# Buffers of a four-layer graph network rearranged: a third residual tile, sums and 32x32 transposes in place, PSUM banks moved to the products

## The chip, the core and the metric

The kernel runs on one core of a Trainium2 chip. TensorE (PE) multiplies matrices into PSUM. VectorE (DVE), ScalarE (ACT) and GpSimd (POOL) do elementwise work; SyncE (SP) issues most transfers. The metric is device time in microseconds, the median of several executions. A profiled execution has its own time span, and is a little shorter than that median.

## The reference

128 samples of 64 tokens with 512 features go through four residual layers, in fp32. Each begins with a layer norm and a relu. Layers 0 and 2 have four heads of width 64, layer 1 has eight and a second layer norm, and layer 3 is a graph step with eight heads.

```python
# layers 0, 2 (and 1 with its own norm, 8 heads)
h = jnp.maximum(_layernorm(x, axis=-1), 0.0)
sim = jnp.einsum('bhid,bhjd->bhij', q, k) * scale       # q, k, v = h @ W
sim = jnp.where(adjacency_mask[:, None, :, :], sim, neg)
attn = jax.nn.softmax(sim, axis=-1)
x = x + (attn @ v) @ Wo + bo
# layer 3
m = embs @ map_w.T + map_b
cos_adj = (cos > THRESHOLD)                              # cosine of the heads of m
p_attn = jax.nn.softmax(where(pad, NEG, q k / sqrt(dk))) # q, k from m
sem_h = embs @ gcn_map_w.T + gcn_map_b
out = relu(((cos_adj * p_attn) @ sem_h) @ gcn_W.T / (sum + 1)); x = x + out
```

## The kernel before, in words

The tokens are cut into 16 groups of 512 (8 samples), and each layer goes over all groups. Between the layers the residual stream lies in device memory. A group's steps are: load, layer norm (`loads`, `layernorms`), turn the tokens so that features lie on partitions (`transposes`, L591), projections, scores and softmax (`front`, `scores` L957), the attention product with v (`attention` L1122, `last` L1270), the output projection, the residual sum and the store.

**Projections** are done with seven half-size products for eight (`winograd`, L700), which takes sums of the quarters of both operands. The sums of the weights are made once. The sums of the tokens are four 128x512 tiles per operand: `sums_of_b` (L356) makes B01−B00, B11 minus that, B11−B01, and B10 minus the second, on GpSimd for h and m, and on VectorE for the attention's output. In the profile they are `t<-hT`, `t<-m` (L366, L363). In the product's code they are T[0] to T[3]. The order of the products is A0·B00, A1·B10, A5·T1, A4·T0, A2·T2, A6·B11, A3·T3. Results land in PSUM tiles called `mA` (ring `ma`) and `mB`, `mC` (ring `mm`), and copies (ACT, L669) and sums (DVE, L682) bring them into SBUF.

**Turning the tokens** goes three ways. Eight groups go through TensorE (`ptr`, L609). 28 groups of layers 0 and 2 have their 32x32 blocks moved by 16 transfers each on SP (`moves`, L556, `F<-xin`), followed by VectorE's 32x32 transposes (`by_vector`, L586). 28 groups of layers 1 and 3 have the blocks copied by ScalarE and GpSimd (`turned_tokens`, L512), with a `t` tile as the staging place, then VectorE's transposes (L546).

**Softmax weights** are turned per unit of a group (`transposed`, L1014): eight 32-partition copies on ScalarE from E to F (L1021), and one VectorE transpose from F to pt (L1026). Then the attention product `po` (64x64 quarters of the array) can run.

**Residuals** (`residuals`, L1056): two halves of a group are loaded to `xres` tiles; GpSimd adds the bias (L1071) and the first product terms `u` (L1087, L1092), VectorE the others (L682), and SP stores them (L1112).

**The order.** Each engine executes one fixed list of instructions, in order; an instruction waits for semaphores of what it reads and of what it overwrites. The list is written when the program is built: each part of the work is a generator that yields an engine and an assumed duration (`pe`, `dve`, `act`, `pool`, `quads`), and `Order.run` (L138) takes next the one that could start first. DRAIN is the assumed time of a change between 64x64 quarters and the full array. A `Ring` or `Bank` with n buffers lets a new tile begin when an older one is released, in the plan as on the chip. So durations and numbers of buffers decide the order on every engine, SP's queue too.

**PSUM** has eight banks: `sc` (scores, one tile of two banks), `ma` 2, `mm` 2, and `tr` 2 for the transposes `ptr`.

Of the kernel before, what the change touches and what calls it, by code (L numbers as in the profile page):

```python
# [24 lines left out]
NEG_L3 = -1e10 * 8  # L25

DRAIN = 0.085


class Event:
# [24 lines left out]
class Stream:  # L74
# [14 lines left out]
    def quads(self):  # L89
        return self.op[3:] == ("quads",)  # L90
# [138 lines left out]
def gnn_stack(ctx: ExitStack, tc: tile.TileContext, a: dict, out: bass.AP):  # L229
# [10 lines left out]
    def bank(tag, n, shape, dtype=F32):  # L240
        return Bank(od, ctx.enter_context(tc.tile_pool(name=tag, bufs=1)), n, shape, dtype, tag)
# [4 lines left out]
    dram = ctx.enter_context(tc.tile_pool(name="dram", bufs=1, space=bass.MemoryType.DRAM))  # L246
    r_w = ring("w", 4, [P, 7, 2, H])
    r_xin = ring("xin", 2, [P, TB, D])
    r_xres = ring("xres", 2, [P, 2, D])
    r_u = bank("u", 4, [P, D])  # L250
    r_h = ring("h", 2, [P, NC, TB * P])
    r_t = bank("t", 3, [P, NC, 2, H])
    r_qk = ring("qk", 3, [P, NC, TB * P])
    r_m = bank("m", 2, [P, NC, TB * P])
    r_v = bank("v", 2, [P, TB, D])
    r_e = ring("e", 2, [P, 16, N])
    r_f = ring("f", 1, [P, 16, N])
    r_c = ring("c", 1, [P, 2, 512], U8)
    r_pt = ring("pt", 1, [P, 16, N])
    r_adj = ring("adj", 2, [P, TB, N], U8)  # L260
    r_n0 = ring("n0", 2, [P, TB, N], U8)
    ps = bass.MemoryType.PSUM
    r_sc = ring("sc", 1, [P, 2, 512], space=ps)
    r_ma = ring("ma", 2, [P, 512], space=ps)
    r_mm = ring("mm", 2, [P, 512], space=ps)
    r_tr = ring("tr", 2, [P, NC, P], space=ps)

    xs = [[dram.tile([TB * P, D], F32, name=f"x{l}_{s}") for s in range(NG)] for l in range(3)]
    x_done = {}
# [85 lines left out]

    def sums_of_b(B, T, vector=False):  # L356

        n = T.shape[2]
        for o, i0, i1 in ((T[:, 0], B(0, 1), B(0, 0)), (T[:, 1], B(1, 1), T[:, 0]),
                          (T[:, 2], B(1, 1), B(0, 1)), (T[:, 3], B(1, 0), T[:, 1])):  # L360
            if vector:
                yield dve(0.9)
                nc.vector.tensor_tensor(o, i0, i1, ALU.subtract)  # L363
            else:
                yield pool(1.42)
                nc.gpsimd.tensor_tensor(o, i0, i1, ALU.subtract)  # L366
# [94 lines left out]

    hT, hB, h_ready, h_done, t_done = {}, {}, {}, {}, {}

    def quarters(v):

        return lambda j, k: v[:, 2 * j:2 * j + 2, k * H:(k + 1) * H]
# [45 lines left out]
    def turned_tokens(l, s):  # L512


        for half in range(2):
            yield n_ready[l, s, half]
        if (l, s) == (3, 1):
            yield o_taken
        h, h_done[l, s] = yield from r_h.new("hT")
        hT[l, s] = h  # L520
        x, xe = normed.pop((l, s))
        T, t_done[l, s] = yield from r_t.new("T")
        F = T.rearrange("p c a n -> p c (a n)")
        xv = x.rearrange("p b (c k f) -> p k c b f", c=NC, k=4)
        Fv = F.rearrange("p c (b i f) -> p i c b f", b=TB, i=4)
        blocks = [(i, k) for k in range(4) for i in range(4)]

        def part(pairs, done):
            for i, k in pairs:
                o, v = Fv[32 * k:32 * (k + 1), i], xv[32 * i:32 * (i + 1), k]  # L530
                if done:
                    yield pool(0.9)
                    nc.gpsimd.tensor_copy(o, v)
                else:
                    yield act(0.615)
                    nc.scalar.copy(o, v)  # L536
            if done:
                done.set()
        moved = od.event()
        od.spawn(part(blocks[:3], moved), 3)  # L540
        yield from part(blocks[3:], None)
        yield moved
        xe.set()
        for c in range(0, NC, 2):
            yield dve(1.25)
            nc.vector.transpose(h[:, c:c + 2, :], F[:, c:c + 2, :])  # L546
        if l == 1:
            for c in range(NC):
                yield act(0.787)
                nc.scalar.activation(h[:, c, :], h[:, c, :], AF.Identity,  # L550
                                     bias=beta[:, c:c + 1], scale=gamma[:, c:c + 1])
        hB[l, s] = (quarters(h), T, od.event())
        h_ready[l, s].set()
        return h

# [35 lines left out]
    def transposes(steps):  # L591

        for l, s in steps:
            if (l, s) in by_dma:
                h = yield from by_vector(l, s)
            elif (l, s) in turned:
                h = yield from turned_tokens(l, s)
            else:
                h, h_done[l, s] = yield from r_h.new("hT")
                hT[l, s] = h  # L600
            for half in range(0 if (l, s) in turned + by_dma else 2):
                yield n_ready[l, s, half]
                x, xe = normed[l, s]
                for t in range(2):
                    b = 2 * half + t
                    pt, pe_ = yield from r_tr.new("ptr")
                    for c in range(NC):
                        yield pe(0.115)
                        nc.tensor.transpose(pt[:, c, :], x[:, b, c * P:(c + 1) * P], ident)  # L609
                    if b == TB - 1:  # L610
                        xe.set()
                    yield act(0.6)
                    nc.scalar.copy(h[:, :, b * P:(b + 1) * P], pt)
                    pe_.set()
                if (l, s, half) == (0, 0, 0):
                    yield from has_h(l, s, h)
            if (l, s) != (0, 0) and (l, s) not in turned:
                yield from has_h(l, s, h)
            yield from sums_of_b(quarters(h), hB[l, s][1], (l, s) == (0, 0))
            hB[l, s][2].set()  # L620
            if (l, s) == (0, 0):
                first_t.set()

    def has_h(l, s, h):
        T, t_done[l, s] = yield from r_t.new("T")
        hB[l, s] = (quarters(h), T, od.event())
        h_ready[l, s].set()


# [70 lines left out]
    def winograd(A, BT, tokens_out, out_, used, begun):  # L700
# [36 lines left out]
        yield read  # L737
        for e in sums:
            yield e
        yield from product(p_, A[:, 5], T[:, 1], tokens_out, False)  # L740
        read, u2 = first(0, 1, p_)
        r_, re_ = yield from r_mm.new("mC")
        r_ = r_[:, 0:width]
        yield from product(r_, A[:, 4], T[:, 0], tokens_out, True)
        read5, c22 = first(1, 1, r_)
        yield read
        yield from product(p_, A[:, 2], T[:, 2], tokens_out, False)
        read, c22 = add(1, 1, p_, c22)
        begun.set()
        yield read5  # L750
# [1 line left out]
        c12 = second(0, 1, r_, u2)  # L752
        od.spawn(when([c12], re_), 0)
        yield read
        yield from product(p_, A[:, 3], T[:, 3], tokens_out, False)
        od.spawn(out_.alone(1, 0, p_, c22, pe_), 0)
        od.spawn(when([*every, pe_], used), 0)

# [94 lines left out]

    def k_part(s, z):
        yield from of_map("k", s, z, k_b)
        od.spawn(when([z["q_ready"], z["k_ready"]], s_ready[3, s], z["m_used"], z["T_done"]), 0)

    def sem_part(s, z):

# [12 lines left out]
    def sums_after(e, B, z, done, last):  # L872
        yield e

        T, z["T_done"] = yield from (r_w if last else r_t).new("mT_T")
        z["T"] = T = T[:, 0:NC]
        yield from sums_of_b(B, T)
        done.set()

# [77 lines left out]
    def scores(lT, rT, npair, blocks):  # L957
        S, e = yield from r_sc.new("sc")
        nb = len(blocks)
        for b, t in enumerate(blocks):  # L960
            for c in range(npair):
                if c % 2 == 0:
                    yield quads(0.235)
                col = slice((c * nb + b) * N, (c * nb + b + 1) * N)
                for g in range(2):
                    k = slice(t * P + g * N, t * P + (g + 1) * N)
                    for par in range(2):
                        r = slice(par * N, (par + 1) * N)
                        nc.tensor.matmul(S[g * N:(g + 1) * N, par, col],  # L969
                                         lT[r, c, k], rT[r, c, k], start=True, stop=True)  # L970
        return S, e
# [41 lines left out]

    def transposed(E, e):  # L1014

        F, fe = yield from r_f.new("F")
        for g in range(2):
            for i in range(2):
                for k in range(2):
                    yield act(0.587)  # L1020
                    nc.scalar.copy(F[g * N + 32 * k:g * N + 32 * (k + 1), :, 32 * i:32 * (i + 1)],  # L1021
                                   E[g * N + 32 * i:g * N + 32 * (i + 1), :, 32 * k:32 * (k + 1)])
        e.set()
        o, oe = yield from r_pt.new("pt")
        yield ("dve", 1.2, 1.0)
        nc.vector.transpose(o, F)  # L1026
        fe.set()
        return o, oe

    def masks(l, s):  # L1030

# [90 lines left out]
    def attention(l, s):  # L1122
# [8 lines left out]
        for u, blocks in enumerate(units):  # L1131
# [3 lines left out]
            for b, t in enumerate(blocks):  # L1135
                for c in range(npair):
                    if c % 2 == 0:
                        yield quads(0.235)
                    for par in range(2):
                        h = 2 * c + par  # L1140
                        for g in range(2):
# [18 lines left out]
        T, te = yield from r_t.new("oT_T")  # L1160
        if (l, s) == (2, NG - 1):
            o_taken.set()
        T = T[:, :, 0:nch, :]
        yield from sums_of_b(ov, T, True)
        yield w_ready[wkey]
        wo = W["o1"] if l == 1 else o_part(W[wkey])
# [103 lines left out]
    def last(s):  # L1270
# [3 lines left out]
        for u in range(2):  # L1274
# [5 lines left out]
            for b in range(2):  # L1280
                t = 2 * u + b
                for i in range(4):
                    yield quads(0.118)
                    for ch in range(2):
                        h = 4 * ch + i
                        c, par = h // 2, h % 2
# [96 lines left out]
```

## Time and profile before

| | |
|---|---|
| time, median of 3 | 2754.21 us (2753.09 to 2754.67) |
| span of the profiled execution | 2750.0 us |
| PE, DVE, ACT, POOL busy | 97%, 71%, 69%, 59% |
| layers, roughly | L0 to 550, L1 to 1400, L2 to 1880, L3 to 2750 us |
| one product of 128x128 weights with 256 columns (two records) | 0.43 us on PE |
| one po or score group (64 quarter records) | 1.09 us between starts |
| one GpSimd token sum, 128x512 | 1.27 us |
| one VectorE transpose, 128x1024 | 1.23 us |
| one ScalarE copy, 32x512 | 0.615 us |

A row of the page or of a timeline reads: start, duration, engine, line, operation, what it writes and reads, and in brackets the idle time before it and the event that ended it. A row of waits has the waiting engine and line, the releaser, total us, times, and the longest. The chain is followed back from the last instruction to what released it.

### The profile page before, as it was taken

The page shows a single profiled execution, that of the slowest core. Times are in us where ns is not written, and L with a number is a line of the kernel's source. Part 1 is how long each engine was busy: PE and PEld are TensorE (multiplying, and loading weights), DVE is VectorE, ACT ScalarE, POOL GpSimd, SP SyncE. Part 2 cuts the span into 40 slices and gives each one's busy share as a digit, 9 for nine tenths or more (in the row PEclk, how much of TensorE's full clock was granted, in tenths as well). Part 3 has the DMA queues.
Part 4 walks back from the last instruction along what each step waited for, and adds up shares of the span by engine and source line. Part 5 has one row for each costly group of instructions (what it writes and reads, how often), then busy time and mean ns, then how long its engine had stood idle before and what let it go on. Part 6 is the DMA issues. An engine that isn't in the chain of part 4 may idle for free.

```text
span 2750.0 us, 63860 instructions
## 1 busy us (share of the span) xinstructions
PE 2678.9 (97%) x26280; PEld 2320.6 (84%) x26280; DVE 1956.6 (71%) x2836; ACT 1889.6 (69%) x3517; POOL 1615.5 (59%) x1242
## 2 busy tenths in 40 slices
PE   7989999999999999999999999999999999999997
PEld 6878888788888888888888888888888888888876
DVE  6777987767666766776668888747776677766656
ACT  5666767677877777777566667666667766677644
POOL 4666777645444544544657677686656565565643
PEclk9999999999999999999999999999999999999998
DMA  5565654212111211112455556423222342223221
GB/s 166 134 150 138 174 140 144 97 48 79 63 47 64 78 48 60 63 66 78 114 145 143 162 148 163 140 93 96 78 65 72 81 101 64 64 71 84 68 64 48
DMA packets 396980, 267.92 MB, mean 97 GB/s; under 512 B 260496, under 2 KB 305552, under 8 KB 396688
## 3 DMA queue, kind: packets, MB, share of 16 engines
q1 hardware_dynamic: 382176, 249.37, 32.8%
q10 hardware_dynamic: 14512, 14.47, 1.6%
q8 instruction: 207, 3.39, 0.5%
q14 instruction: 85, 0.70, 0.1%
HBM read 166.77 MB, written 67.63 MB: 85 GB/s over the span
## 4 chain that ended last, share of the span: by engine, by line
PE 91%; DVE 4%; ACT 2%; DMA 1%; SPq 1%; POOL 1%; issue 1%; POOLq 0%; ACTq 0%; DVEq 0%
PE mA L652 46%; PE mC L652 23%; PE mB L652 12%; PE sc L969 5%; PE po L1144 2%; PE po L1289 1%; ACT F L1021 1%; SPq L571 1%; PE mmn L911 1%; DVE mx L986 0%; PE ptr L609 0%; DMA F<-xin 0%; ACT E L992 0%; DVE st L443 0%; DVE sc L980 0%
## 5 line engine op out<-in xcount | busy, mean ns | idle before, releaser
L1021 ACT COPY F<-E 32x512 f32<-32x512 f32 x768 | 472.6, 615 | 46.1 <-POOL E L1012 28.7
L1092 POOL TENSOR_TENSOR xres<-xres,u 128x512 f32<-128x512 f32 x192 | 255.8, 1341 | 234.1 <-ACT u L1087 203.7
L1071 POOL TENSOR_TENSOR xres<-xres,u 128x512 f32<-128x512 f32 x192 | 266.2, 1407 | 55.5 <-DMA xres<-x 33.9
L366 POOL TENSOR_TENSOR t<-hT 128x512 f32<-128x512 f32 x126 | 178.5, 1416 | 167.7 <-DVE hT L546 89.6
L459 ACT ACTIVATE xin<-xin,rs 128x512 f32<-128x512 f32 x320 | 248.5, 812 | 12.1 <-DVE rs L452 9.2
L536 ACT COPY t<-xin 32x512 f32<-32x512 f32 x364 | 224.1, 616 | 6.4
L443 DVE BATCH_NORM_STATS2 st<-xin 128x6 f32<-128x512 f32 x320 | 214.4, 670 | 8.3 <-DMA xin<-in_x 4.0
L652 PE MATMUL mA<-w_vo,t 128*128 128x128 f32 (+1 forms) x1152 | 206.0, 315 | 7.3 <-ACT u L1087 4.5
L669 ACT COPY v<-mA 128x256 f32<-128x256 f32 (+1 forms) x192 | 93.6, 488 | 168.2 <-PE mA L652 163.3
L450 POOL TENSOR_TENSOR rs<-rs,mhalf 128x2 f32<-128x2 f32 x160 | 115.6, 726 | 147.8 <-DVE rs L448 118.2
L1012 POOL TENSOR_TENSOR E<-E,sm 128x1024 f32<-128x1024 f32 x64 | 129.3, 2020 | 117.2 <-DVE sm L1010 84.1
L652 PE MATMUL mA<-t,w_qk 128*128 128x256 f32 x768 | 183.1, 380 | 2.5 <-DVE t L363 1.4
L652 PEld LDWEIGHTS mA<-w_vo,t 128*128 128x128 f32 x1152 | 164.8, 193 | 20.5 <-ACT u L1087 6.3
L366 POOL TENSOR_TENSOR t<-hT,t 128x512 f32<-128x512 f32 x126 | 175.5, 1393 | 8.0 <-DVE hT L546 4.2
L652 PE MATMUL mA<-t,w_q 128*128 128x256 f32 x744 | 179.6, 384 | 0.0
L652 PE MATMUL mA<-t,w_k 128*128 128x256 f32 x744 | 177.5, 381 | 0.0
L652 PEld LDWEIGHTS mA<-t,w_qk 128*128 128x128 f32 x768 | 144.6, 190 | 22.7 <-DVE t L363 1.6
L1006 DVE TENSOR_REDUCE sm<-E 128x16 f32<-128x1024 f32 x128 | 154.8, 1209 | 8.8 <-ACT E L999 6.7
L652 PEld LDWEIGHTS mA<-t,w_q 128*128 128x128 f32 x744 | 140.7, 191 | 20.7 <-issue 0.8
L1087 ACT COPY u<-mA 128x512 f32<-128x512 f32 x144 | 84.4, 586 | 106.9 <-PE mA L652 105.4
L652 PEld LDWEIGHTS mA<-t,w_k 128*128 128x128 f32 x744 | 140.2, 190 | 19.4
L1026 DVE STREAM_TRANSPOSE pt<-F 128x1024 f32<-128x1024 f32 x96 | 118.6, 1235 | 41.2 <-ACT F L1021 40.9
(220 smaller groups left out, 6883.5 us busy)
## 6 DMA issues: line engine op xcount, KB each, us to landing
x<-xres SPq DMA_DIRECT2D x96, 512.0 KB
xin<-x SPq DMA_DIRECT2D x96, 512.0 KB
xres<-x SPq DMA_DIRECT2D x64, 512.0 KB
F<-xin SPq DMA_DIRECT2D x448, 64.0 KB
xres<-in_x SPq DMA_DIRECT2D x32, 512.0 KB
u<-rs SPq DMA_DIRECT2D x128, 128.0 KB
xres<-x SPq DMA_DIRECT2D x64, 256.0 KB
out<-xres SPq DMA_DIRECT2D x64, 256.0 KB
```

What stands on the lines that cost most here:

```text
L366: nc.gpsimd.tensor_tensor(o, i0, i1, ALU.subtract)
L443: nc.vector.bn_stats(st, v[:, t, :])
L459: nc.scalar.activation(v[:, t, :], v[:, t, :], func, bias=rs[:, 2, t:t + 1], scale=rs[:, 0, t:t + 1])
L536: nc.scalar.copy(o, v)
L652: nc.tensor.matmul(o, l, r, start=(first and m == 0 and k == 0), stop=(k == KC - 1), skip_group_check=True)
L969: nc.tensor.matmul(S[g * N:(g + 1) * N, par, col], lT[r, c, k], rT[r, c, k], start=True, stop=True)
L1006: nc.vector.tensor_reduce(o, E, AX.X, ALU.add)
L1012: nc.gpsimd.tensor_mul(E, E, sm[:, :, None].to_broadcast([P, 16, N]))
L1021: nc.scalar.copy(F[g * N + 32 * k:g * N + 32 * (k + 1), :, 32 * i:32 * (i + 1)], E[g * N + 32 * i:g * N + 32 * (i + 1), :, 32 * k:32 * (k ...
L1026: nc.vector.transpose(o, F)
L1071: nc.gpsimd.tensor_add(xr[:, t, :], xr[:, t, :], bo[l])
L1092: nc.gpsimd.tensor_add(v, v, both(u))
```

## The change

All arithmetic stays. The tiles are placed differently.

- `xres` has three buffers instead of two.
- `sums_of_b` makes B11−B01 last, and for h and the attention's output puts it into the place of the quarter B01, which no product reads (`with_room`). `t` tiles hold three sums instead of four. For m of layer 3, whose quarters are still read, the sum goes to a tile of its own, `t2`, with one buffer, released after the k product (`k_part`).
- `turned_tokens` copies the blocks straight into h, and the 32x32 transposes run in place.
- The softmax's F and pt are one tile: the transpose runs in place, and there are two of them.
- In PSUM `tr` goes; `ma` and `mm` have three banks each, and `ptr` takes its banks from `mm`.
- The planner's assumed durations change: DRAIN .085 to .1, the quarter groups .235 to .242 and .118 to .121.

```diff
-DRAIN = 0.085
+DRAIN = 0.1
...
-    r_xres = ring("xres", 2, [P, 2, D])
+    r_xres = ring("xres", 3, [P, 2, D])
-    r_t = bank("t", 3, [P, NC, 2, H])
+    r_t = bank("t", 3, [P, 3, 2, H])
+    r_t2 = ring("t2", 1, [P, 2, H])
-    r_f = ring("f", 1, [P, 16, N])
-    r_pt = ring("pt", 1, [P, 16, N])
+    r_pt = ring("pt", 2, [P, 16, N])
-    r_ma = ring("ma", 2, [P, 512], space=ps)
-    r_mm = ring("mm", 2, [P, 512], space=ps)
-    r_tr = ring("tr", 2, [P, NC, P], space=ps)
+    r_ma = ring("ma", 3, [P, 512], space=ps)
+    r_mm = ring("mm", 3, [P, 512], space=ps)
...
-        for o, i0, i1 in ((T[:, 0], B(0, 1), B(0, 0)), (T[:, 1], B(1, 1), T[:, 0]),
-                          (T[:, 2], B(1, 1), B(0, 1)), (T[:, 3], B(1, 0), T[:, 1])):
+        for o, i0, i1 in ((T[0], B(0, 1), B(0, 0)), (T[1], B(1, 1), T[0]),
+                          (T[3], B(1, 0), T[1]), (T[2], B(1, 1), B(0, 1))):
...
+    def with_room(T, B):
+        return [T[:, 0], T[:, 1], B(0, 1), T[:, 2]]
...
-        Fv = F.rearrange("p c (b i f) -> p i c b f", b=TB, i=4)
+        Fv = h.rearrange("p c (b i f) -> p i c b f", b=TB, i=4)
...
-            nc.vector.transpose(h[:, c:c + 2, :], F[:, c:c + 2, :])
+            nc.vector.transpose(h[:, c:c + 2, :], h[:, c:c + 2, :])
...
-        hB[l, s] = (quarters(h), T, od.event())
+        hB[l, s] = (quarters(h), with_room(T, quarters(h)), od.event())
...
-                    pt, pe_ = yield from r_tr.new("ptr")
+                    pt, pe_ = yield from r_mm.new("ptr")
+                    pt = pt.rearrange("p (c n) -> p c n", c=NC)
...
-        od.spawn(when([z["q_ready"], z["k_ready"]], s_ready[3, s], z["m_used"], z["T_done"]), 0)
+        od.spawn(when([z["q_ready"], z["k_ready"]], s_ready[3, s], z["m_used"], z["T_done"], z["t2_done"]), 0)
...
-        z["T"] = T = T[:, 0:NC]
+        t2, z["t2_done"] = yield from r_t2.new("mT_T2")
+        z["T"] = T = [T[:, 0], T[:, 1], t2, T[:, 2]]
...
-                    yield quads(0.235)
+                    yield quads(0.242)
...
-        F, fe = yield from r_f.new("F")
+        F, fe = yield from r_pt.new("F")
...
-        o, oe = yield from r_pt.new("pt")
         yield ("dve", 1.2, 1.0)
-        nc.vector.transpose(o, F)
-        fe.set()
-        return o, oe
+        nc.vector.transpose(F, F)
+        return F, fe
...
-        T = T[:, :, 0:nch, :]
+        T = with_room(T[:, :, 0:nch, :], ov)
...
-                    yield quads(0.118)
+                    yield quads(0.121)
```

More of the change, by code (lines that the diff above doesn't have):

```diff
@@ L356, in sums_of_b @@
     def sums_of_b(B, T, vector=False):
-        n = T.shape[2]
-        for o, i0, i1 in ((T[:, 0], B(0, 1), B(0, 0)), (T[:, 1], B(1, 1), T[:, 0]),
-                          (T[:, 2], B(1, 1), B(0, 1)), (T[:, 3], B(1, 0), T[:, 1])):
+        for o, i0, i1 in ((T[0], B(0, 1), B(0, 0)), (T[1], B(1, 1), T[0]),
+                          (T[3], B(1, 0), T[1]), (T[2], B(1, 1), B(0, 1))):
             if vector:
@@ L522, in turned_tokens @@
         T, t_done[l, s] = yield from r_t.new("T")
-        F = T.rearrange("p c a n -> p c (a n)")
         xv = x.rearrange("p b (c k f) -> p k c b f", c=NC, k=4)
-        Fv = F.rearrange("p c (b i f) -> p i c b f", b=TB, i=4)
+        Fv = h.rearrange("p c (b i f) -> p i c b f", b=TB, i=4)
         blocks = [(i, k) for k in range(4) for i in range(4)]
@@ L625, in has_h @@
         T, t_done[l, s] = yield from r_t.new("T")
-        hB[l, s] = (quarters(h), T, od.event())
+        hB[l, s] = (quarters(h), with_room(T, quarters(h)), od.event())
         h_ready[l, s].set()
@@ L739, in winograd @@
             yield e
-        yield from product(p_, A[:, 5], T[:, 1], tokens_out, False)
+        yield from product(p_, A[:, 5], T[1], tokens_out, False)
         read, u2 = first(0, 1, p_)
@@ L743, in winograd @@
         r_ = r_[:, 0:width]
-        yield from product(r_, A[:, 4], T[:, 0], tokens_out, True)
+        yield from product(r_, A[:, 4], T[0], tokens_out, True)
         read5, c22 = first(1, 1, r_)
         yield read
-        yield from product(p_, A[:, 2], T[:, 2], tokens_out, False)
+        yield from product(p_, A[:, 2], T[2], tokens_out, False)
         read, c22 = add(1, 1, p_, c22)
@@ L754, in winograd @@
         yield read
-        yield from product(p_, A[:, 3], T[:, 3], tokens_out, False)
+        yield from product(p_, A[:, 3], T[3], tokens_out, False)
         od.spawn(out_.alone(1, 0, p_, c22, pe_), 0)
@@ L1137, in attention @@
                     if c % 2 == 0:
-                        yield quads(0.235)
+                        yield quads(0.242)
                     for par in range(2):
```

## The prediction

> **What bounds the kernel.** I read the page's busy shares, the slices and the chain that ended last, then the windows by stage, and then TensorE's waits.
>
> ```profile
> span 2750.0 us, 63860 instructions
> PE 2678.9 (97%) x26280; PEld 2320.6 (84%) x26280; DVE 1956.6 (71%) x2836; ACT 1889.6 (69%) x3517; POOL 1615.5 (59%) x1242
> ...
> PEclk9999999999999999999999999999999999999998
> ...
> PE 91%; DVE 4%; ACT 2%; DMA 1%; SPq 1%; POOL 1%; issue 1%; POOLq 0%; ACTq 0%; DVEq 0%
> ```
>
> TensorE is busy for 97% at nearly full clock, and 91% of the last chain is its own work. So only what changes TensorE's idle time, or the ends of the span, can move the time. The windows (core's share, PE busy first) say where it idles:
>
> ```profile
> 50.00:690.00 640.00, 613.04 (x5822) 539.60 (x5821) 492.69 (x734) 443.44 (x887) 414.59 (x324) 0.98 0.45 124
> 700.00:1390.00 690.00, 689.80 (x6226) 599.20 (x6225) 466.13 (x695) 517.58 (x828) 334.10 (x280) 1.00 0.21 67
> 1390.00:2080.00 690.00, 681.58 (x6634) 593.91 (x6634) 506.59 (x735) 466.11 (x965) 479.25 (x357) 1.00 0.45 124
> 2080.00:2700.00 620.00, 617.12 (x6652) 521.45 (x6650) 420.10 (x550) 407.25 (x741) 343.14 (x242) 0.99 0.28 72
> 2700.00:2750.00 50.00, 31.16 (x603) 26.52 (x602) 32.54 (x35) 22.16 (x35) 20.11 (x13) 0.79 0.26 65
> ```
>
> Layer 1 has 0.2 us idle in 690: nothing to win there. Layer 0 and its passage to layer 1 have 27 us, the passage to layer 3 8.4, the tail 19. The waits of TensorE:
>
> ```profile
> PE po L1289 <- DVE pt L1026: 10.7, 2, 5.8
> PE mC L652 <- ACT v L669: 5.8, 2, 5.1
> PE po L1144 <- DVE mv L445: 5.4, 1, 5.4
> PE mA L652 <- DVE hT L586: 5.2, 1, 5.2
> PE mA L652 <- ACT u L1087: 4.5, 1, 4.5
> ```
>
> The timeline places them. The 5.2 is at 67 us, where the instruction orders of the two kernels are still equal. At 160.37 a product waits for the copy `u`, behind softmax copies on ScalarE; at 199.95 another waits for copy `v`, behind seven such copies. At 536.74 the second attention product waits for its transposed weights (its named releaser had long ended; the transpose at 535.35 is the last):
>
> ```profile
> 526.52 1.19 DVE L1026 STREAM_TRANSPOSE pt<-F 128x1024 f32<-128x1024 f32 x1
> 529.82 1.88 ACT L1021 COPY F<-E 32x512 f32<-32x512 f32 x3 [2.69 <-DVE rs L448]
> 532.20 3.12 ACT L1021 COPY F<-E 32x512 f32<-32x512 f32 x5
> 535.35 1.25 DVE L1026 STREAM_TRANSPOSE pt<-F 128x1024 f32<-128x1024 f32 x1 [1.06 <-ACT F L1021]
> 536.74 1.98 PE L1144 MATMUL po<-pt,v 64*64 64x64 f32 x64 [5.38 <-DVE mv L445]
> ```
>
> With a single F, the eight copies of the second unit cannot begin before the first transpose has read it.
>
> **What the Trainium skill says.** "TensorE: Matmul & The Clock Gate", The mechanism: matrix multiplies keep program order, at start and end. The trace agrees: behind the po at 536.74 the next `mA` starts only at 538.66. So a late operand delays everything, and the written order is what counts. "PSUM — Partial Sum Buffer", The four PSUM rules: one matmul's output lies in one bank, 512 fp32 columns. Both kernels hold all eight; the trace cannot show the limit, but shows waits for a free product bank: `mB` 1.66 us at 189.93, `mmf` 2.25 at 1412.22. "SBUF — State Buffer", Who interferes with whom: a VectorE instruction with two SBUF inputs contends with a GpSimd one that reads SBUF. The trace agrees: the L363 sum at 155.44, beside GpSimd's E at 155.27, took 2.01 us, where its like takes 0.41. New orders may make or break such meetings; I price them in the slips below.
>
> **The change, part by part.** Instruction counts per engine and kind are equal in both programs (13206 on TensorE, 2838 VectorE, 3554 ScalarE, 1247 GpSimd, 1184 SyncE), and so are the 442 switches between 64x64 groups and full products. TensorE's own work is unchanged: 0.
>
> *In-place transposes and sums.* The same 96 + 56 VectorE transposes (1.23 us each), and the same GpSimd sums (1.27 us) to another address. No row shows the in-place form. Bounds: 0, or if it drained for 0.3 us more, 152 x 0.3 = 46 us on VectorE, which is 29% idle; on the path only where a wait already ends at such a transpose (few, under 2 us). I take 0. The sums' third and fourth change places (T3 before T2): the product with T2 comes before that with T3, so T2 comes one sum, 1.3 us, later against its product. GpSimd idles 41%, and no wait above ends at a sum: 0, or 1.3 us at a layer's start.
>
> *Third product banks, transposes moved into `mm`.* Takes away the bank waits 1.66 (189.93), 0.69 (227.78), 0.90 and 2.25 (1405, 1412) as far as order allows. In exchange the `ptr` transposes (128 records, so 8 token groups of 16; four banks in each group) share `mm` with `mB`/`mC`: each holds a bank for 0.6 us of TensorE and 0.6 of ScalarE, a third bank covers that; if not, some 0.6 us a bank, 32 x 0.6 = 19 us at the very worst. I take 0.
>
> *F and pt as two in-place buffers.* The second unit's copies can begin 5 us earlier; the two po are now 16 matmuls apart (16 x 0.43 = 6.9 us) where they were 4.
>
> *The order.* The planner's constants and buffers change what is written where. TensorE's orders agree to about 154 us; from there layer 0 is rearranged (next group's q·k product ahead of the output projection; po about 4.75 us earlier), to the passage at ~550. Layer 1 differs little, layer 2 takes on the same pattern, layer 3 is nearly equal up to its last two groups.
>
> Walk through 150–230. Removed: 4.66+1.66+5.24+0.69 = 12.25. In the new order the hT transposes come earlier on VectorE, but the fetched F lands at 153.6, leaving about 2.1 for hT and 3.0 for the same `u`: 5.1. Net −7.2.
> Passage 430–550. Removed: 1.56 (441) + 0.56 + 5.45 = 7.57; left 0.5. Net −7.1.
> Passage to layer 2, 1400–1415: 3.15 removed, I leave 1.0. Net −2.1.
> New slips in the rearranged 150–570: from 1390 to 2620 this kernel's stalls over 0.6 us sum to 11.6 us in 1230, 0.0094 per us; x 420 = +4.0.
>
> *The tail.* `t2` has one buffer, so the fourth sum of the last group waits for the product of group 14's k that reads it, and the planner now puts the score products of both units of group 14 back to back after k, before the last q. Before, they were spread through q:
>
> ```profile
> 2665.91 1.46 PE L652 MATMUL mA<-m,w_q 128*128 128x256 f32 x6
> 2667.30 1.16 PE L969 MATMUL sc<-kT,qT 64*64 64x64 f32 x64
> ...
> 2668.53 1.34 DVE L980 COPY_PREDICATED sc<-adj,negs 128x1024 f32<-128x1024 uint8 x1 [3.45 <-PE sc L969]
> ...
> 2669.91 1.22 DVE L986 TENSOR_REDUCE mx<-sc 128x16 f32<-128x1024 f32 x1
> ...
> 2671.89 1.21 DVE L996 TENSOR_TENSOR E<-sc,mx 128x1024 f32<-128x1024 f32 x1
> ```
>
> The `sc` ring stays at one buffer. The first unit waits for kT's last evacuation (about 1.05 us after 2665.9), the second for mask, maximum and subtraction (1.34+1.22+1.21 = 3.8 and hops of 0.35): about 5.2 us with nothing else allowed to pass. Also one po (1.28 us with its switches) now stands ahead of the last semantic products instead of in the idle tail. What follows them keeps its length: GpSimd's E and four adds of v (1.9 + 5.2 us), eight copies, transpose, po. So the end moves by 5.2 to 5.2 + 1.28 = 6.5, as far as the po was hidden; I take +5.7.
>
> Stores on SyncE: the residual store moves from after twelve of a group's sixteen F moves to after three, costed at 0 because F moves take 16 x 0.63 = 10 us of a 27 us group; see the second rival.
>
> Sum: −7.2−7.1−2.1+4.0+5.7 = −6.7. Span 2750.0 − 6.7 = 2743.3. The profiled run's span lies 4.2 us under the median 2754.2, so 2747.5.
>
> **Rivals.** *One for one: within 0.2%* (5.5 us, about what can be told from no change here). The new layer 0 slips as the old did: 19.8 us of stalls in its 150–550. With slips of 10 instead of 4 us, the time is 2753.5. For it: `u` still stands behind softmax copies near 160, and F still arrives at 153.6. Against it: layer 2 already runs this pattern of po and projection, with almost no stall.
>
> *Slower, by SyncE's head of line.* A store issues only when the residual is finished, and everything behind it in the queue stands; at 103.9–121.4 SyncE stood 17 us at one. Now thirteen F moves (8.2 us) and the next load of xin come behind it. Per group of layer 0 and 2 after its start (some 26) any overshoot over the slack of 27 − 10 − about 5 for other transfers = 12 us comes as TensorE waiting for hT. It cancels the gain at 6.7/26 = 0.26 us of overshoot per group, and shows as slower from (6.7 + 5.5)/26 = 0.47; at 0.65 it costs 26 x 0.65 = 16.9, which gives 2747.5 + 16.9 = 2764. For it: the third residual buffer lets the store fall later in the order. Against: only one hT wait (5.2) in all of before, at the start.
>
> *The claimed gain is larger.* The walks' 5.1 left-over and slips stay out: −6.7−9 gives 2738.
>
> *Nothing of it reaches the bound:* TensorE idles too little; then the stalls stay as they are, and the tail alone gives 2754.2 + 5.7 = 2760, the edge of slower.
>
> **Numbers.** Forecast and the larger gain: 0.45 (faster). One for one: 0.33, from 2749 to 2759. SyncE's case, or the tail with no gain before it: 0.22. Likeliest 2747.5; 8 in 10 within 2738 to 2762, from the larger gain to just inside the SyncE case. The likeliest case's own range is 2740 to 2751.
>
> **What would show it.** Right: no stall over 1 us at 530–545 and at 185–205; mm-bank waits gone; PE busy within 2 us of 2679; a gap of about 4 us between two `sc` groups near 2660 with both score groups adjacent. Wrong: waits of `mA` for hT L586 in several groups with a store ahead on SyncE (second rival); in-place transposes clearly over 1.23 us; new waits for `t`, `mm` or `v` in layer 0 worth more than 5 us.

## The result, and the profile after

The changed kernel takes 2750.03 us (median of 20 runs, 2744.29 to 2756.89) beside 2754.26 us for the kernel before (20 runs, 2749.51 to 2761.38). The ratio is 0.9987, with a 95% interval of 0.9980 to 0.9994. It is faster, by 4.2 us between the medians: less than the 0.2% at which the prediction called a difference clear, and 2.5 us over its likeliest value of 2747.5.

The page of the changed kernel: span, busy shares, granted clock and the chain.

```profile
span 2750.6 us, 63739 instructions
...
PE 2682.1 (98%) x26280; PEld 2323.4 (84%) x26280; DVE 1950.9 (71%) x2836; ACT 1885.3 (69%) x3517; POOL 1608.4 (58%) x1242
...
PEclk9999999999999999999999999999999999999998
...
PE 84%; DVE 7%; ACT 3%; POOL 3%; DMA 2%; issue 1%; SPq 0%; ACTq 0%; DVEq 0%; POOLq 0%
```

The profiled execution took 2752.83 us, 2.8 us over this kernel's median, and its span of 2750.6 us is no shorter than the 2750.0 of before. The execution profiled before was on the quick side: its span is 4.2 us under the median, where spans in the other runs are about 2 us under the time of the same execution, so it was some 2 us faster than usual (an estimate). So the two traces don't show the 4 us as a sum; they show where time was won and given back. The windows of the changed kernel, cut as those of before:

```profile
50.00:690.00 640.00, 623.87 (x5946) 549.27 (x5945) 501.90 (x746) 453.27 (x907) 419.54 (x330) 0.99 0.47 125
700.00:1390.00 690.00, 685.66 (x6187) 593.87 (x6186) 438.61 (x683) 507.13 (x803) 339.28 (x281) 1.00 0.23 74
1390.00:2080.00 690.00, 683.16 (x6641) 596.87 (x6641) 524.08 (x738) 469.84 (x981) 465.21 (x349) 1.00 0.44 118
2080.00:2700.00 620.00, 611.80 (x6613) 516.89 (x6613) 419.27 (x547) 402.23 (x733) 347.35 (x243) 0.99 0.28 71
2700.00:2750.00 50.00, 31.48 (x549) 26.38 (x547) 29.23 (x34) 20.07 (x32) 13.65 (x10) 0.82 0.25 64
```

TensorE's busy time rose from 613.0 to 623.9 of the 640 us between 50 and 690, and fell from 617.1 to 611.8 in the stretch to 2700. (Busy counts half-clock time too.) TensorE's waits now:

```profile
PE po L1272 <- DVE F L1010: 10.0, 1, 10.0
PE mA L636 <- ACT v L653: 7.0, 14, 1.6
PE sc L954 <- DVE E L981: 6.9, 4, 4.9
PE mA L636 <- DVE hT L569: 6.0, 1, 6.0
PE mA L636 <- ACT u L1070: 3.6, 3, 1.7
```

The 5.2 us for `v`, 5.4 for po and 4.5 for `u` are gone. In their place are many short waits for `v` (14 with 7.0 us) and one of 4.9 us between two score groups. The 10.0 us at the end stands where two waits made 10.7.

Two notes on counting. Single waits of TensorE are given below from start to start, less the usual spacing, except where a view beside them shows the number; the views count from the modelled end of the last record and show up to 0.2 us less. And the x of a row counts matmul records, of which a product on the full array has two: x8 is four products, and the "8 products" of an expectation below are eight records.

For an account in places, I compare the moment at which each trace's TensorE has done the same amount of matmul work. Both do the same work, so the difference is idle or half-clock time. One entry is good to about 1 us, since it depends on what runs at the cut. The changed kernel's lead changes like this (minus is time won):

| stretch, time of before | predicted | in the profiled pair |
|---|---|---|
| 150–250 | −7.2 | −13.7 |
| 250–530 | +4.0 | +6.3 |
| 530–565, passage to layer 1 | −7.1 | −7.5 |
| 565–1300 | 0 | +0.7 |
| 1300–1455, passage to layer 2 | −2.1 | +2.3 |
| 1455–1740 | 0 | +2.5 |
| 1740–2660 | 0 | +1.7 |
| 2660 to the end | +5.7 | +7.9 |

Before 2660 the changed kernel is 7.2 us ahead; at the end it is level.

### The profile page after: what moved, and what is told of

The parts are those of the page before. It is cut to its first block, busy times and chain, and to the rows that moved or that the text cites. A ratio compares the mean times of both kernels' runs of the same rounds, so it can differ in the third digit from the quotient of the medians.

```text
span 2750.6 us, 63739 instructions
## 1 busy us (share of the span) xinstructions
PE 2682.1 (98%) x26280; PEld 2323.4 (84%) x26280; DVE 1950.9 (71%) x2836; ACT 1885.3 (69%) x3517; POOL 1608.4 (58%) x1242
## 4 chain that ended last, share of the span: by engine, by line
PE 84%; DVE 7%; ACT 3%; POOL 3%; DMA 2%; issue 1%; SPq 0%; ACTq 0%; DVEq 0%; POOLq 0%
PE mA L636 43%; PE mC L636 21%; PE mB L636 11%; PE sc L954 4%; PE po L1127 2%; PE po L1272 1%; ACT F L1006 1%; ACT E L977 1%; DVE sc L965 1%; DVE mx L971 1%; PE mmn L896 1%; POOL t L346 1%; DVE st L423 1%; POOL E L997 0%; PE ptr L593 0%
## 5 line engine op out<-in xcount | busy, mean ns | idle before, releaser
L439 ACT ACTIVATE xin<-xin,rs 128x512 f32<-128x512 f32 x320 | 248.4, 812 | 22.5 <-DVE rs L432 20.3
L519 ACT COPY hT<-xin 32x512 f32<-32x512 f32 x364 | 224.1, 616 | 6.4
L346 POOL TENSOR_TENSOR t<-hT 128x512 f32<-128x512 f32 x63 | 80.7, 1281 | 168.8 <-DVE hT L529 96.2
L1010 DVE STREAM_TRANSPOSE F<-F 128x1024 f32<-128x1024 f32 x96 | 118.4, 1234 | 60.6 <-ACT F L1006 60.6
L977 ACT ACTIVATE E<-sc,mx 128x64 f32<-128x64 f32 x512 | 124.9, 362 | 32.7 <-DVE mx L974 32.7
L516 POOL COPY hT<-xin 32x512 f32<-32x512 f32 x84 | 64.4, 766 | 138.1 <-ACT xin L439 135.8
L636 PE MATMUL mA<-w_vo,t 128*128 128x128 f32 (+1 forms) x768 | 135.4, 312 | 8.1 <-ACT v L653 4.2
L636 PE MATMUL mA<-hT,w_qk 128*128 128x256 f32 x512 | 129.3, 392 | 7.5 <-DVE hT L569 6.0
L997 POOL TENSOR_TENSOR E<-E,f 128x1024 f32<-128x1024 f32 x32 | 61.1, 1910 | 111.7 <-DVE f L995 95.0
L636 PE MATMUL mA<-t,w_qk 128*128 128x256 f32 x512 | 122.7, 380 | 1.4 <-DVE t L343 1.4
L869 POOL TENSOR_TENSOR v<-v,gcn_row 128x512 f32<-128x512 f32 x64 | 81.2, 1300 | 71.9 <-ACT v L653 71.9
```

Source lines behind the costliest of these rows:

```text
L439: nc.scalar.activation(v[:, t, :], v[:, t, :], func, bias=rs[:, 2, t:t + 1], scale=rs[:, 0, t:t + 1])
L636: nc.tensor.matmul(o, l, r, start=(first and m == 0 and k == 0), stop=(k == KC - 1), skip_group_check=True)
L977: nc.scalar.activation(E[:, i, :], S3[:, i, :], AF.Exp, bias=mx[:, i:i + 1], scale=0.125)
L997: nc.gpsimd.tensor_mul(E, E, sm[:, :, None].to_broadcast([P, 16, N]))
L1010: nc.vector.transpose(F, F)
```

## The experiments

Each was timed in several rounds beside the kernel before on the same chip, whose medians were 2754.3 to 2756.0 us. "Ahead" is in the sense of the table, from the profile.

**The tail.** The timeline of the changed kernel's TensorE:

```profile
2659.42 1.18 PE L954 MATMUL sc<-kT,qT 64*64 64x64 f32 x48 [0.17 <-ACT kT L657]
2665.54 1.99 PE L954 MATMUL sc<-kT,qT 64*64 64x64 f32 x64 [4.95 <-DVE E L981]
2667.46 3.72 PE L636 MATMUL mA<-m,w_q 128*128 128x256 f32 x8
```

The predicted gap is there. What the prediction had not counted is that the work after it is slow: a score group of 1.16 us takes 1.99, and eight records that otherwise end 1.89 us after their start take 3.72. The first experiment removes the wait.

```diff
-        t2, z["t2_done"] = yield from r_t2.new("mT_T2")
+        if last:
+            t2, z["t2_done"] = T[:, 3], od.event()
+        else:
+            t2, z["t2_done"] = yield from r_t2.new("mT_T2")
```

> The changed kernel, except that the last group's fourth sum of m lies in the free fourth quarter of its own tile, so that it no longer waits for the one t2 tile. Theory (t2 sets the tail): the two score groups of group 14 part again, the wait of 5.2 us between them goes, and with it the half clock after it (8 products in 3.55 us where 1.73 is usual, a score group in 1.99 instead of 1.16: 2.6 us): 7 to 8 us less than the changed kernel, about 2742.5. Rival (GpSimd's rows of v and the last E set the end, whatever PE does before): within 2 us of the changed kernel, 2748 to 2751.

Measured: 2745.34 us (ratio 0.9965, 0.9953 to 0.9977). The score groups part again, both stalls go, and from 2660 to the last semantic product nothing is lost against the kernel before (7.3 us ahead at 2633, 7.3 at 2711, where the changed kernel went from 7.2 ahead to 0.8 behind). Against the changed kernel the ratio fell by 0.0022, some 6 us, a little less than expected, and the two intervals leave room for 7 to 8. The theory holds for the place; the price is measured once more, with the old durations, at the end of this section.

The second leaves the wait but fills it.

```diff
+            if (l, s, u) == (3, NG - 2, 1):
+                warm, we = yield from r_mm.new("warm")
+                for _ in range(9):
+                    yield pe(0.43)
+                    nc.tensor.matmul(warm[:, 0:H], ident, gcn_row[:, 0:H], start=True, stop=True)
+                we.set()
             S, se = yield from scores(z["q"], z["k"], 2 * nch, blocks)
```

> The changed kernel with nine products on constants (3.9 us) put between the two score groups of group 14; the wait for the softmax stays, PE is busy in it. Theory (PE's clock halves after about 3 us of idleness): the score group after it takes 1.16 us and the next eight products 1.73 instead of 1.99 and 3.55; 2.5 us less than the changed kernel, about 2747.5. Rival (the slow stretch is from something else, such as the transfers then under way): both stay slow, and the time is 2750.

```profile
2659.58 4.15 PE L1205 MATMUL warm<-gcn_row,ident 128*128 128x256 f32 x18
2664.60 1.16 PE L954 MATMUL sc<-kT,qT 64*64 64x64 f32 x64 [0.87 <-DVE E L981]
2665.69 1.99 PE L636 MATMUL mA<-m,w_q 128*128 128x256 f32 x8
```

The score group starts as late after the first as before (6.13 us against 6.12), but now takes 1.16 us and the eight records 1.99. So the slow stretch follows from TensorE's idleness, not from the work that it waited for. That is 2.6 us in this place. The time, 2749.85 us (0.9984, 0.9977 to 0.9991), lies below the changed kernel's ratio by less than either interval; the timeline decides here, not the time.

**Buffers or order.** Old durations with the new buffers, and new durations with the old buffers:

```diff
-DRAIN = 0.1
+DRAIN = 0.085
-                    yield quads(0.242)
+                    yield quads(0.235)
-                    yield quads(0.121)
+                    yield quads(0.118)
```

> The changed kernel with the assumed durations of the kernel before (0.085, 0.235, 0.118), so its own buffers in another order. Theory (buffers give the gain): no wait of po over 1 us in the passage from layer 0 to 1, PE waits over 4 us absent from 150 to 230; 2750 plus or minus 3. Rival (the order which the new durations write gives it): the waits of 4.7 and 5.2 us on ScalarE's u and v in layer 0 come back, each with 2 us of half clock: 2757 or more.

Measured: 2750.26 us (0.9980, 0.9973 to 0.9988). It is 11.7 us ahead at 223, as the changed kernel is (12.3). The passage has one wait of 2.5 us, for q and not of po, and layer 0 one of 3.1 at 299. The large waits stay away without the new durations.

> The kernel before with the assumed durations of the changed one (0.1, 0.242, 0.121), so old buffers in another order. Theory (buffers give the gain): the wait of 5.4 us of the second po for its single F at the passage to layer 1 stays, as does at least one of the waits of 4 to 5 us in layer 0; the tail is as before; 2752 to 2757. Rival (durations give it): these waits go without the buffers, and with the unhurt tail it takes about 2742 to 2745.

Measured: 2757.17 us (1.0007, 0.9999 to 1.0015). The waits of 4.7 and 4.1 us of layer 0 are there. But the wait of po at the passage is not: the two po start at 538.10 and 546.73 with other products in all of the time between, with one F and one pt. That part of the expectation, and the cause that the prediction gave for it, is refuted. Waits elsewhere took the gain away again: 3.3 us for a product bank at 504, and near 1380 2.8 us for the load of the folded weights.

**One part undone.** Three kernels undo one buffer each in the changed kernel:

```diff
-    r_pt = ring("pt", 2, [P, 16, N])
+    r_pt = ring("pt", 1, [P, 16, N])
```

> The changed kernel with one in-place tile for F and its transpose instead of two. Theory (the second F tile took away the wait at the passage to layer 1): copies of the second unit now wait even for the first unit's po, so a wait of po of 5 us or more, with 2 us of half clock, comes back near 530, perhaps in layer 1 too: 2755 to 2762. Rival (the new order alone spaces the po): no po wait over 1 us, 2750 plus or minus 3.

Measured: 2769.07 us (1.0043, 1.0031 to 1.0056). Slower than both views said, and not where the theory said: at the passage no po waits at all (528.76 and 540.84), and in layer 1 one waits 2.2 us, at 581. The cost is a wait of 4.9 us for `u` at 679 with half clock, about 6 us at the passage to layer 2, and some 20 us in the tail, where the changed kernel lost 8: with one F a unit's copies start only after the po before. Two F tiles are needed once the transpose is in place, but they are not what cleared the passage.

```diff
-    r_ma = ring("ma", 3, [P, 512], space=ps)
-    r_mm = ring("mm", 3, [P, 512], space=ps)
+    r_ma = ring("ma", 2, [P, 512], space=ps)
+    r_mm = ring("mm", 2, [P, 512], space=ps)
+    r_tr = ring("tr", 2, [P, 512], space=ps)
```

> The changed kernel with the old share of PSUM (two banks for mA, two for mB and mC, two for the transposes). Theory (third banks cut some waits of 0.7 to 2.3 us and no more): 2751 to 2755, with waits of mB or mmf on VectorE's sum of the bank before again. Rival (the banks are the main gain, since order follows from them): the waits of 4 to 5 us of layer 0 come back, 2757 or more. A third view, no effect at all: 2750.

Measured: 2755.71 us (1.0000, 0.9991 to 1.0010). Layer 0 keeps its gain (12.4 us ahead at 223). The ratio is 0.0013, some 3.6 us, over the changed kernel's, and the time a little over the first theory's range. The trace loses in several places: 290, the passage to layer 2 (4.3 us at 1372), layer 2. But the 4.3 us is a wait for the load of the folded weights, and its trace shows no wait of `mB` or `mmf` for a sum of VectorE, which the theory named. So the rival is out and the size is near the theory's, but its mechanism is not shown.

```diff
-    r_xres = ring("xres", 3, [P, 2, D])
+    r_xres = ring("xres", 2, [P, 2, D])
```

> The changed kernel with two residual tiles. Theory (the residual loads are off TensorE's path, as in the prediction): within 3 us of the changed kernel, 2747 to 2753, no wait of PE behind xres or u over 3 us. Rival (the third tile is what took away the wait of 4.7 us for u at 160, since u is added into xres): that wait is back, with half clock, 2755 or more.

Measured: 2780.48 us (1.0095, 1.0081 to 1.0109). The prediction's theory falls. The wait of 4.66 us for `u` at 160 is back to the hundredth, and others with it, up to 24 us behind the kernel before at 530. The trace shows how the residual reaches TensorE. GpSimd and TensorE at 223–234:

```profile
223.08 2.48 POOL L1054 TENSOR_TENSOR xres<-xres,u 128x512 f32<-128x512 f32 x2 [4.12 <-DMA xres<-in_x]
...
232.27 2.61 POOL L346 TENSOR_TENSOR t<-hT,t 128x512 f32<-128x512 f32 x2
...
233.59 2.93 PE L636 MATMUL mA<-t,w_qk 128*128 128x256 f32 x6 [7.05 <-POOL t L346]
```

With two tiles a half's load is issued only when an older half is stored. GpSimd stands 4.1 us at the bias add for it, the token sums stand behind it in the same queue, and TensorE stands 7.05 us for the sums. The kernel before has this wait too: there GpSimd stands 20.3 us for such loads between 150 and 540, in this kernel 26.9, in the changed one 7.6.

**The third residual tile alone.** Own F and pt, own banks and the old durations, with the in-place sums and token transposes, and three or two residual tiles. The space comes from the sums: three `t` tiles of three sums instead of four free 6 KB of each partition, of which t2 takes 2 and the third residual tile 4.

```diff
-    r_xres = ring("xres", 2, [P, 2, D])
+    r_xres = ring("xres", 3, [P, 2, D])
     # other buffers and durations as before; sums and hT in place, t2 with one buffer
```

> The kernel before with the in-place sums and token transposes and the third residual tile, but with its own F and pt, PSUM banks and assumed durations. Theory (the third residual tile by itself takes the waits out of layer 0): at 160 PE waits under 2 us for u, nothing over 4 us between 150 and 250, PE about 12 us ahead of the kernel before at 250; with the tail's 8 us from t2 and slips of some 4, about 2752. Rival (it takes the other parts too): the waits of 4.7 and 5.2 us are there, PE less than 4 us ahead at 250; 2758 or more.

> The same with two residual tiles. Theory (third tile decides): the wait of 4.7 us for u at 160 is there, PE under 4 us ahead at 250 or behind, and about 10 us slower than with three tiles, 2760 to 2766. Rival (the other rearrangements brought the gain): as with three tiles, 2750 to 2754.

With three: 2747.89 us (0.9978, 0.9971 to 0.9986). With two: 2764.08 us (1.0034, 1.0022 to 1.0046). The windows 150 to 250 of the two, three first:

```profile
150.00:250.00 100.00, 97.06 (x948) 86.49 (x948) 87.73 (x131) 67.79 (x149) 74.56 (x59) 1.00 0.70 167
```

```profile
150.00:250.00 100.00, 88.31 (x825) 78.28 (x824) 72.95 (x110) 57.59 (x124) 69.87 (x55) 0.95 0.65 165
```

With two tiles this stretch is that of the kernel before (88.41 us busy, 825 records against 821); with three it is that of the changed kernel (96.96). With two, the waits of 4.66, 1.76 and 5.23 us in layer 0 and 5.17 us of po at the passage are all there; with three, one of 1.83 at 161 remains in that stretch, and no wait of po at the passage (523.38 and 532.00, the time between filled). So in this pair, which differs in nothing else, the third residual tile made both gains. It did so through the order. TensorE at 160, with two tiles and with three:

```profile
156.47 1.03 PE L638 MATMUL mB<-w_vo,m 128*128 128x256 f32 x4
161.99 2.07 PE L638 MATMUL mA<-w_vo,t 128*128 128x256 f32 x4 [4.50 <-ACT u L1074]
```

```profile
154.18 1.89 PE L638 MATMUL mA<-hT,w_qk 128*128 128x256 f32 x8
155.91 1.89 PE L638 MATMUL mB<-hT,w_qk 128*128 128x256 f32 x8
157.64 1.03 PE L638 MATMUL mA<-w_vo,m 128*128 128x256 f32 x4
158.50 1.03 PE L638 MATMUL mB<-w_vo,m 128*128 128x256 f32 x4
161.20 1.13 PE L638 MATMUL mA<-w_vo,t 128*128 128x256 f32 x4 [1.67 <-ACT u L1074]
```

The copy `u` comes no more than 0.8 us earlier, but with three tiles sixteen records of the next group's q·k stand ahead of those that wait for it. The changed kernel and its version with two tiles part at the same place. At the passage the new durations alone had spaced the two po as well. The kernel with three is 17.5 us ahead from 614 to 1375, more than the changed kernel (14.4 at 563, 13.7 at 1300), and loses 9 us of it in layer 2 and 8 in the tail. In the two timings the changed kernel and this one stand so close (0.9980 to 0.9994 and 0.9971 to 0.9986) that their order stays open.

**The slips in layers 0 and 2.** In the changed order ScalarE copies `v` out of PSUM after three exponentials of the next softmax, and these wait for VectorE's mask. In the changed kernel's timeline:

```profile
367.30 4.82 POOL L1075 TENSOR_TENSOR xres<-xres,u 128x512 f32<-128x512 f32 x3
367.36 2.30 DVE L965 COPY_PREDICATED sc<-n,negs 128x1024 f32<-128x1024 uint8 x1
...
373.22 1.16 PE L636 MATMUL mA<-w_vo,t 128*128 128x128 f32 x8 [1.50 <-ACT v L653]
```

The mask usually takes 1.22 us. Six kernels have this order: the changed one, t2 in the weights, the filled gap, one F, the old banks and the later fold. In their groups between 250 and 540 and between 1470 and 1760, 22 of the 23 masks over 2.1 us have a wait of 1.5 to 2.4 us at this product after them, and none of the 86 under 1.3 has one over 0.32. In the case shown GpSimd had begun 0.06 us earlier; in the group one period before, the mask began first, at 339.29, and took 1.22 us. The Trainium skill's "SBUF — State Buffer", Who interferes with whom, says that a VectorE instruction with two inputs in SBUF contends with a GpSimd one that reads SBUF, and that the one that begins second is blocked until the first is done. It doesn't name this instruction, whose mask and fill value are in SBUF. The traces agree. Of the 36 masks over 1.3 us, 35 took 1.09 us plus what was left of the GpSimd add under way when they began (2.30 = 1.09 + 1.21). The other way round, 71 adds that GpSimd began up to 0.86 us after a mask took 2.34 us less that delay, where 1.27 is usual.

So the durations show what holds up the mask, though no run removed it. It is not all of the loss. Between 245 and 535 the changed kernel's TensorE is idle for 5.9 us, of which 3.9 are waits for copies of `v` behind exponentials, and one of them, of 1.5 us, follows a mask over 2.1 us. Which groups are hit differs from kernel to kernel with the same order (2 in the changed kernel's trace, 5 in the first experiment's).

An attempt to write `v` ahead and to let the fold's load arrive has both edits below; a second one has that of the load alone. Both keep the last sum in its own tile:

```diff
-        yield dve(1.5)
+        yield dve(2.4 if narrow else 1.5)
         nc.vector.copy_predicated(...)
-        yield ("actq", 0.5, 7.0)
+        yield ("actq", 0.5, 12.0)
         nc.scalar.dma_start(raw, ...)
```

> The kernel with the last sum in its own tile, and two assumed durations longer: the mask of layers 0 and 2 at 2.4 us instead of 1.5, and the load for the folded weights at 12 us instead of 7. In the changed kernel ScalarE's copy of v is written behind three exponentials; where GpSimd holds up the mask (2.30 us instead of 1.22), PE waits 1.6 us for v. Theory (these slips are that meeting): v is copied before the exponentials again, the waits of mA for v over 1 us go, 6 to 8 us; and the product on the folded weights no longer waits 2.7 us for its load: 2733 to 2740. Rival (another order brings other slips of the same size): 2743 to 2748.

Measured: 2752.22 us (0.9987, 0.9977 to 0.9997). The time is outside both ranges, some 6 us over the kernel with the last sum in its own tile. The rival is right in kind: six waits of 1.2 to 1.7 us, mostly for another copy of `v` (L673), stand in layer 0 between 209 and 408 in their place, and three more in layer 2. A longer assumed duration moved the waits instead of removing them, and this run can't say what they had cost.

> The kernel with the last sum in its own tile, and the load for the folded weights assumed at 12 us instead of 7, which moves only the fold's products near 1365. Theory (PE's wait of 2.7 us there, and the 1.5 us of half clock after it, are on the path): the wait goes and 4 us with it, 2741 plus or minus 2. Rival (what is won there is lost by the new place of the fold): 2744 to 2746.

Measured: 2744.80 us (0.9957, 0.9945 to 0.9969). The wait for the load is gone, and a wait of 2.35 us of po for F stands at 1366 with half clock after it. The stretch 1360 to 1380 has 17.72 us busy at a clock of 0.91, where the first experiment had 17.42 at 1.00. So the half clock that the theory wanted to save was not there in the first experiment, only in the changed kernel's trace. No gain: the rival, as far as this place tells.

**The best one.** The first experiment's edit with the old durations:

> The last sum in its own tile, with the assumed durations of the kernel before. Theory (the tail's 8 us and the order of layer 0 are independent): the gap between the two score groups is gone, 7 to 8 us less than the changed kernel with old durations, 2742 to 2743. Rival (the tail is worth only the 5 us that the first such run showed): 2745.

Measured: 2742.28 us (five runs, 2740.20 to 2743.58; 0.9953, 0.9942 to 0.9965), 8.0 us under the same kernel with the single t2 by the medians, 7.4 by the ratios. The tail's price is 8 us here and was some 6 with the new durations; the profile of the changed kernel says 7.9. This beats both kernels: 12.8 us under the kernel before by the medians of its own comparison. It has the three residual tiles and no gap between the score groups, and its layer 2 has no wait of TensorE over 1 us.

## Why the prediction was right or wrong

*What bounds the kernel, and the unchanged work:* right. The in-place operations cost what the others did: 1.23 us per transpose (96 of F, median 1.234), 1.27 us per fourth sum (63 of h, median 1.272).

*150 to 250:* right in direction, half in size, and only in part right in cause. The walk left 5.1 us of waits where 3.1 are left. And no step counted the half clock: with it, 4.66 us of waiting at 160 cost about 2 us more (four records took 2.08 us where 1.03 is usual, and those after them were slow too). The new order, the next group's q·k ahead of the output projection, was read rightly. What wrote it is the third residual tile, for which the sum had no term; the bank step is not needed for it, since the old banks keep 12.4 us of lead at 223.

*The passage to layer 1:* right in size (−7.1, measured −7.5), and right that the two po would stand further apart. Wrong in what it laid this on: the step "F and pt as two in-place buffers" is refuted by three kernels with one F and no such wait (new durations; three residual tiles alone; one F). The distance of the two po in the written order did it. The single F sets the wait only where they stand close: five products apart in the kernel before, where the prediction counted four, against 17, 17 and 25 in these.

*New slips, +4.0:* the density of the old order was too mild for the new. The stretch 250–530 cost 6.3 us, and layer 2 another 2.5, which the sum put at nothing. The larger part of the waits, those for `v` behind exponentials, could have been read: ScalarE's new order was there to see, and so was the mask's range of durations, which makes a few of them long.

*The passage to layer 2:* wrong sign (−2.1, measured +2.3). The old bank waits went, and a wait of 2.7 us for the fold's load came, with half clock after it in this trace. The bank step named what was removed and not that the fold's products would now come before their own load.

*The tail:* the mechanism was right, place and length (5.2 us predicted, 5.16 measured). The missing term is the half clock, 2.6 us; 5.7 became 7.9.

*Stores on SyncE, costed at nothing:* right; no wait of several groups for hT is in the profile, so the second rival did not happen. The time, 2750.0, lies between the forecast's 2747.5 and the 2753.5 of the middle rival, slips as large as before's, and inside the range of both; it doesn't tell them apart. The sum of −6.7 against −4.2 us is closer than its terms deserved. The gains were put at 16.4 us and are 21.2 in the traces; the losses were put at 9.7 and are 21.4. By the traces the two cancel, and the sum is some 7 us off. That the medians put it only 2.5 us off is luck: the two profiled executions lie on opposite sides of theirs.

## What to carry to other kernels

Undo each part of a rearrangement before believing its most visible part: here the residual tile, far from TensorE, gave the gain through GpSimd's queue and the order. When instructions are in fixed lists, ask of each moved copy what now stands ahead of it and how long that can take at worst, not on average. And price a stall of the matrix engine of some 4 us or more with the slow clock that follows, and one of 2 to 4 us with the chance of it.

## What the runs showed that I had not expected

After idleness TensorE can run at half speed for a while. A gap of 5.16 us was followed by eight records in 3.55 us between starts where 1.73 is usual. "TensorE: Matmul & The Clock Gate" in the Trainium skill, What's actually happening, describes it: half clock after about 3.4 us of idleness, watched in a window that runs freely. The traces agree that the same gap can be followed by either clock. They don't agree that it takes 3.4 us. The same wait for the fold's load, first in the kernel with the last sum in its own tile, then in the one with the filled gap:

```profile
1365.84 1.13 PE L396 MATMUL mmf<-bdw,raw 128*128 128x128 f32 x8 [2.58 <-DMA raw<-in_gcn]
```

```profile
1367.55 2.05 PE L396 MATMUL mmf<-bdw,raw 128*128 128x128 f32 x8 [2.73 <-DMA raw<-in_gcn]
```

The first went on at full clock, the second at 0.50 over 3 us. With two residual tiles a gap of 2.64 us at 316 was followed by a clock of 0.55 and one of 3.33 at 352 by 1.00. After the start of the program, every gap of 3.97 us or more in the 14 traces was followed by half clock; of the 43 from 2 to 3.4 us 29 were. So between these lengths the length alone doesn't decide.

One buffer was worth about 15 or 30 us, depending on what else was changed: with the new F tiles, banks and durations, a third residual tile moved the ratio from 1.0095 to 0.9987; with the old ones, from 1.0034 to 0.9978.
